# Decoder block on one core: in the opening stage, the first half's gates move behind three of its four query projections, and four idle products are put ahead of the first transposes

## The chip, the cores and the metric

The kernel runs on one core of a Trainium2 chip. The metric is the device time of one execution in microseconds (us), the median over several executions. The engines of the core that matter here are TensorE (PE in the profile; its weight loads are PEld), VectorE (DVE), ScalarE (ACT), GpSimd (POOL) and SyncE (SP, which issues most DMAs). Each runs its own instructions strictly in the order in which the program issues them to it, and waits for the others through semaphores.

## The reference

One pre-norm decoder layer with three residual branches, in float32, for x of 4 x 1024 x 512 and a context of 4 x 1024 x 384, with 16 heads of 32:

```python
x = x + attn(layernorm(x))            # "phase 0" of the kernel
x = x + xattn(layernorm(x), ctx)      # "phase 1"
x = x + ffn(layernorm(x))

# attn, the part that matters here (x is already normalized):
aperture   = sigmoid(x @ Wa + ba)     # 512 -> 16, one gate per query and head
expression = sigmoid(x @ We + be)     # 512 -> 16, one gate per key and head
inner = x @ Wi ;  outer = x @ Wo ;  v = x @ Wv        # 512 -> 512 each: queries, keys, values
a = softmax(inner . outer / sqrt(32))
a = a * aperture[query] * expression[key] ;  a = a / (a.sum + 1e-8)
y = ((a @ v), rotated and scaled by head) @ Wout
```

Only the preparation of the first of the four batches (its normalization, transposition, gates and projections) is in question. Everything after it is computed as before.

## The kernel before

The work is cut into eight units: phase 0 (self-attention) for the four batches, then phase 1 (cross-attention and feed-forward) for the four. Every unit handles 1024 tokens in two halves of 512 (`hf` = 0 and 1). `pre(u)` makes the preparation of a unit as lists of small steps: `x` (load a half of the input), `ln` (layernorm of a half), `xT` (load it back transposed), `tr` (finish the transposition), `k`, `q`, `v` (projections; the keys use the weight named Wo, the queries Wi, the values Wv), `g` (gates) and `gt` (transposition of the gates). `attention(u, hf)` gives the main steps of a unit (scores, exponentials, product with the values), and `run` mixes the preparation of the next unit between them. No scheduler reorders anything: the order of the lists is the order of each engine's queue (`tc.manual_schedule`).

The first unit has no attention to be mixed into, so its preparation runs alone. It is the list `first`, at the end of `moderate_path`, and that is the place of the change. Its steps, in the order of before:

- `p["x"][0]`: the first half of batch 0, `x0`, whose loads are issued at the very start (L137), with the four quarters of the key weights (`wk0`). `by_quarters` (L92) loads a 512 x 512 weight as four DMAs of 256 KB, one for each slice `c` of the contraction; a projection takes the slices in the order 0 to 3.
- `p["ln"][0]`: layernorm in place on `x0`: statistics (L392, L393), reciprocal root by integer arithmetic (`rsqrt`, L286 to L295), and the four normalizations (L299), one for each tile of 128 tokens. All on DVE.
- `p["x"][1]`: the load of the second half (L374). Ahead of it POOL copies a few values of the first half's root into the target (L373), so the load starts only when the root is there.
- `ahead(0, "q")`, `load_gates`, `ahead(0, "v")`, `load_biases`: the loads of Wi, of the gates' weights (`wae`, eight DMAs of 8 KB; `nbae`, eight small ones), and of Wv on SP's queue, in this order, and the biases and feed-forward weights on POOL's queue.
- `p["tr"][0]`: the first half is transposed on TensorE, by products with the identity (`across`, L321), and copied back by DVE (L280). It is the only half so treated. Every later half goes by DRAM: `away` writes the normalized rows (L303, `rows_d`), `back` reads them with rows and columns exchanged in blocks (L308, `xT`), and DVE transposes within the blocks (L314).
- `p["k"][0]`, then `negate` (DVE changes the sign of the gates' bias `nbae`, L152) and `p["g"][0]`: the gates. 16 small products (L467) with `wae`, the exponential on ACT (L473), one addition on DVE (L474), and four writes of the apertures to DRAM (L476, `iap_d`).
- `weave(p["ln"][1], p["q"][0])`: the four groups of the first half's queries (`proj`, products at L87), with the steps of the second half's layernorm set evenly between them. The two writes of `rows_d` (L303) are part of this layernorm.
- `p["gt"][0]`: SP reads the apertures back (L484, `iap`; it must wait for `iap_d`), PE transposes the gates (L488), DVE takes reciprocals (L493).
- `p["xT"][1]`: SP's four loads of the second half's transposed rows (L308); they wait for `rows_d`.
- `p["v"][0][0:3] + p["tr"][1] + p["v"][0][3:]`: the values of the first half (L87), with DVE's transpositions (L314) of the second half behind the third of four.
- `p["k"][1]`, `p["g"][1]`, `p["q"][1]` and `p["v"][1]`: the same for the second half, then the first attention step (L570).

A projection of one group of 128 columns is 16 products (32 matmul records); its result lies in one of two PSUM banks (`bank()`, a pool of two), so a third group waits until the first was copied out.

Of the kernel before, what the change touches and what calls it, by code (L numbers as in the profile page):

```python
# [42 lines left out]
@with_exitstack  # L43
def decoder_kernel(ctx: ExitStack, tc: tile.TileContext, a: dict, out: bass.AP):

    nc = tc.nc
    keep = ctx.enter_context(tc.tile_pool(name="keep", bufs=1))
    flag = keep.tile([1, 1], I32, name="flag")
    E = mybir.EngineType
    with tc.manual_schedule(engines={E.PE, E.DVE, E.Activation, E.Pool, E.SP}):
        moderate_path(tc, a, out, flag)
    again = nc.values_load(flag[0:1, 0:1], min_val=0, max_val=1, skip_runtime_bounds_check_because="0 or 1")
    with tc.If(again > 0):  # L60
        general_path(tc, a, out)


def moderate_path(tc: tile.TileContext, a: dict, out: bass.AP, flag: bass.AP):
    nc = tc.nc
    x = a["x"]
    with ExitStack() as st:
# [12 lines left out]
        def bank():  # L80
            return pf.tile([P, HALF], F32, tag="f", name="f")
# [22 lines left out]
        ident = const.tile([P, P], F32, name="ident")  # L104
# [28 lines left out]
        x0 = p2.tile([P, 4, D], F32, tag="inT", name="xin")  # L133
# [780 lines left out]
        def weave(light, items):  # L914

            first, second = sum(light, []), sum(items, [])
            out, done = [], 0
            for n, f in enumerate(first):
                upto = (2 * n + 1) * len(second) // (2 * len(first))
                out += second[done:upto] + [f]  # L920
                done = upto
            return [out + second[done:]]
# [20 lines left out]
        def one(f):  # L943
            return [[(0, f)]]
# [4 lines left out]
        def ahead(u, what):  # L949

            return one(lambda: pres[u]["load"](what))
# [62 lines left out]

        p = pres[0]
        S[0]["wk"] = wk0
        first = p["x"][0] + p["ln"][0] + p["x"][1] + ahead(0, "q") + one(load_gates) + ahead(0, "v") + one(load_biases)
        first += p["tr"][0] + p["k"][0] + one(negate) + p["g"][0]
        first += weave(p["ln"][1], p["q"][0]) + p["gt"][0] + p["xT"][1] + p["v"][0][0:3] + p["tr"][1] + p["v"][0][3:]
        first += p["k"][1] + pres[1]["x"][0] + one(load_rotations) + ahead(1, "k") + p["g"][1]  # L1020
        first += weave(pres[1]["ln"][0], p["q"][1][0:3]) + pres[1]["xT"][0] + one(angles) + p["q"][1][3:]
        first += one(load_wout) + one(rotations) + p["gt"][1]
# [15 lines left out]
        o, ln, b, tr, s = ([part for item in tail[k] for part in item] for k in ("o", "ln", "b", "tr", "s"))  # L1038
# [670 lines left out]
```

## Time and profile before

| | |
|---|---|
| time, median of 3 runs | 2247.48 us (2246.14 to 2248.22) |
| the profiled execution | 2244.28 us |
| its span in the profile | 2242.5 us |
| mean granted TensorE clock | 0.992 |
| PE busy | 2185.6 us, 97% of the span |
| DVE busy | 1569.7 us, 70% |
| ACT busy | 1238.0 us, 55% |
| first projection (keys, first half) starts | 17.87 us |
| first gates start on PE | 40.28 us |
| keys of the second half start on PE | 72.22 us |
| first scores (L570) | 115.59 us |

A row of a timeline gives the start and the length of a group of like instructions on one engine, its line, operation, tiles (out<-in) and shape, how many there were, and in brackets how long the engine was idle ahead of them and what ended the wait. A row of the stretches' table gives, for a stretch of the span, its length and mean idle-free time of each engine with the number of instructions, the TensorE clock that was granted (1.00 is full speed), the mean busy share of the 16 DMA engines, and the rate in GB/s. The trace also holds the moment at which each DMA's semaphore was raised by each DMA engine that took part in it; where the text speaks of a landing, it is the last of these. An SP row is the issue of a transfer, not its landing.

### The profile page before, as it was taken

What the parts mean: (1) busy time and instruction counts of PE and PEld (TensorE: products, weight loads), DVE (VectorE), ACT (ScalarE), POOL (GpSimd) and SP (SyncE); (2) the same over time, 40 slices, a digit from 0 to 9 for tenths busy, and PEclk for the clock granted to TensorE, in tenths of its full rate; (3) what the DMA queues carried; (4) which work ended last, traced back from release to release, by engine and by line L of the source; (5) the groups of instructions that cost most, each with busy time, mean ns of one, the idle gap of its engine ahead of it and who ended that gap; (6) DMA issues with size and microseconds to landing.
All of it is one profiled execution on the core that took longest, in us unless ns stands there. A gap on an engine that the chain in (4) does not pass through costs nothing.

```text
span 2242.5 us, 52755 instructions
## 1 busy us (share of the span) xinstructions
PE 2185.6 (97%) x22590; PEld 552.0 (25%) x22590; DVE 1569.7 (70%) x2498; ACT 1238.0 (55%) x1488; POOL 143.5 (6%) x145
## 2 busy tenths in 40 slices
PE   6999999999999999999999999999999999999995
PEld 2322222222222222222222222222222222222222
DVE  3468676797766967567686666868777787856576
ACT  0055545555455554555556565565756566577673
POOL 4000011000000000000000000101000010101010
PEclk9999999999999999999999999999999999999997
DMA  4422223122231221211413032221223142203131
GB/s 112 134 80 50 69 89 106 34 79 69 88 104 35 78 69 46 71 52 41 120 32 104 33 86 63 77 82 45 77 80 103 44 105 68 78 21 102 34 87 40
DMA packets 153305, 161.71 MB, mean 72 GB/s; under 512 B 46202, under 2 KB 91898, under 8 KB 151908
## 3 DMA queue, kind: packets, MB, share of 16 engines
q1 hardware_dynamic: 150380, 156.20, 23.9%
q8 instruction: 179, 2.93, 0.6%
q0 software_dynamic: 2144, 0.98, 0.3%
q10 hardware_dynamic: 536, 1.05, 0.1%
q14 instruction: 66, 0.54, 0.1%
HBM read 115.40 MB, written 42.74 MB: 71 GB/s over the span
## 4 chain that ended last, share of the span: by engine, by line
PE 85%; DVE 6%; ACT 3%; issue 2%; DMA 2%; SPq 1%; DVEq 0%; ACTq 0%; POOL 0%
PE f L87 32%; PE s L570 23%; PE av L597 19%; PE sm L605 6%; DVE es L583 3%; PE sm L627 3%; ACT e L575 2%; SPq L92 1%; DVE g L860 1%; PE f L871 1%; PE f L837 1%; ACT hid L854 1%; DMA sum_d<-both 1%; DMA rec_d<-rec 0%; DVE xT L314 0%
## 5 line engine op out<-in xcount | busy, mean ns | idle before, releaser
L575 ACT ACTIVATE e<-s 128x1024 f32<-128x1024 f32 x1024 | 994.2, 1022 | 716.9 <-PE s L570 534.5
L583 DVE TENSOR_TENSOR es<-es,e 128x1024 f32<-128x1024 f32 x534 | 653.6, 1249 | 277.1 <-ACT e L575 276.6
L570 PE MATMUL s<-q,k 32*64 32x512 f32 x8192 | 620.7, 613 | 7.1 <-ACT e L575 5.4
L597 PE MATMUL av<-e,v 128*32 128x512 f32 x4096 | 554.1, 603 | 0.0
L87 PE MATMUL f<-xT,w 128*32 128x512 f32 x2816 | 331.5, 592 | 0.0
L591 DVE SCALAR_TENSOR_TENSOR eg<-e,sw,eg 128x512 f32<-128x512 f32 x448 | 318.5, 746 | 2.3
L570 PEld LDWEIGHTS s<-q,k 32*64 32x64 f32 x8192 | 136.9, 129 | 459.9 <-ACT e L575 256.6
L581 DVE TENSOR_TENSOR es<-e 128x1024 f32<-128x1024 f32 x89 | 109.5, 1253 | 189.3 <-ACT e L575 181.6
L87 PE MATMUL f<-w,q 128*32 128x512 f32 x1984 | 238.2, 592 | 0.4 <-DVE q L716 0.4
L597 PEld LDWEIGHTS av<-e,v 128*32 128x32 f32 x4096 | 88.5, 108 | 403.8 <-issue 401.1
L87 PEld LDWEIGHTS f<-xT,w 128*32 128x32 f32 x2816 | 92.8, 110 | 210.7 <-issue 203.2
L605 PE MATMUL sm<-e,sw 128*2 128x512 f32 x1024 | 133.3, 592 | 0.0
L774 POOL TENSOR_TENSOR r<-res,bo_bc 128x512 f32<-128x512 f32 x32 | 40.9, 1278 | 1085.2 <-DVE res L766 823.1
L87 PE MATMUL f<-w,xT 128*32 128x512 f32 x896 | 104.9, 592 | 0.6 <-DVE q L280 0.6
L87 PEld LDWEIGHTS f<-w,q 128*32 128x32 f32 x1984 | 65.4, 110 | 149.6 <-issue 143.8
L87 PE MATMUL f<-ctxT,w 128*32 128x512 f32 x768 | 92.3, 592 | 0.0
L87 PE MATMUL f<-w,ctxT 128*32 128x512 f32 x768 | 91.9, 592 | 0.0
L854 ACT ACTIVATE hid<-sT,units 128x256 f32<-128x256 f32 x128 | 76.2, 603 | 23.0 <-DVE g L860 20.2
L627 PE MATMUL sm<-es,ones 128*1 128x512 f32 x348 | 69.0, 591 | 3.9 <-DVE es L583 3.6
L822 POOL TENSOR_TENSOR res<-res,bout_bc 128x512 f32<-128x512 f32 x28 | 59.6, 2136 | 76.9 <-DVE r L299 76.9
L860 DVE SCALAR_TENSOR_TENSOR g<-hid,units,g 128x256 f32<-128x256 f32 x120 | 57.6, 480 | 9.2 <-ACT hid L854 3.8
L677 DVE TENSOR_TENSOR q<-both,recb 128x512 f32<-128x512 f32 x63 | 46.3, 735 | 25.0 <-DMA recb<-rec_d 24.8
(254 smaller groups left out, 1064.9 us busy)
## 6 DMA issues: line engine op xcount, KB each, us to landing
recb<-rec_d SPq DMA_DIRECT2D x252, 64.0 KB
xT<-rows_d SPq DMA_DIRECT2D x60, 256.0 KB
rows_d<-r SPq DMA_DIRECT2D x60, 256.0 KB
w<-in_xattn_Wo SPq DMA_DIRECT2D x9, 1024.0 KB
w<-wout_d SPq DMA_DIRECT2D x8, 1024.0 KB
res<-in_x SPq DMA_DIRECT2D x32, 256.0 KB
x1b_d<-r SPq DMA_DIRECT2D x32, 256.0 KB
res<-x1b_d SPq DMA_DIRECT2D x32, 256.0 KB
```

Source lines behind the costliest of these rows:

```text
L87: nc.tensor.matmul(to[r], lhsT=lhsT[:, j, :] if len(lhsT.shape) == 3 else lhsT[:, r], rhs=rhs, **flags)
L570: nc.tensor.matmul(s[m : m + 64, j, :], lhsT=k[r, g, kt * P + m : kt * P + m + 64], rhs=q[r, g, :], start=True, stop=True,)
L575: nc.scalar.activation(e, s, AF.Exp, scale=SCALE)
L581: nc.vector.tensor_tensor(me["es"][i], me["e", 0][i], es[i], ALU.add)
L583: nc.vector.tensor_tensor(me["es"][i], me["es"][i], es[i], ALU.add)
L591: nc.vector.scalar_tensor_tensor(eg, es[0][:, h, :], gate(kt), eg, ALU.mult, ALU.add)
L597: nc.tensor.matmul(av[r, :], lhsT=me["v"][:, kt, HG * g + h, :], rhs=es[h // 2][:, h % 2, :], start=(kt == 0), stop=(kt == NT - 1),)
L605: nc.tensor.matmul(sm[j * DH : j * DH + sums, :], lhsT=me["sw"][:, t, HG * g + 2 + h, :] if ph == 0 else ones, rhs=me["e", t][1][:, h, :], ...
L627: nc.tensor.matmul(sm[j * DH : j * DH + 1, :], lhsT=ones, rhs=e, start=True, stop=True)
L822: return lambda: nc.gpsimd.tensor_tensor(res[t], res[t], bout_bc, ALU.add)
L854: nc.scalar.activation(hid, res["s"], AF.Relu, bias=units[:, 1, h : h + 1], scale=units[:, 0, h : h + 1])
L860: nc.vector.scalar_tensor_tensor(res["g"], res["hid"], units[:, 2, h - 1 : h], res["g"], ALU.mult, ALU.add)
```

## The change

Two edits in the list `first`. The gates of the first half (`negate` and `g[0]`) are moved behind the third of the four query groups; all steps of the second half's layernorm, which were spread over four query groups, are now spread over these three, so they all stand ahead of `negate` and `g[0]`. The fourth query group follows the gates. And a new step `warm` stands between the load of `x0` and its layernorm: four products of the identity with the raw tiles of `x0`, into a PSUM bank that nobody reads.

```diff
         p = pres[0]
         S[0]["wk"] = wk0
-        first = p["x"][0] + p["ln"][0] + p["x"][1] + ahead(0, "q") + one(load_gates) + ahead(0, "v") + one(load_biases)
-        first += p["tr"][0] + p["k"][0] + one(negate) + p["g"][0]
-        first += weave(p["ln"][1], p["q"][0]) + p["gt"][0] + p["xT"][1] + p["v"][0][0:3] + p["tr"][1] + p["v"][0][3:]
+
+        def warm():
+
+            idle = bank()
+            for i in range(4):
+                nc.tensor.matmul(idle, lhsT=ident, rhs=x0[:, i, :], start=True, stop=True)
+
+        first = p["x"][0] + one(warm) + p["ln"][0] + p["x"][1] + ahead(0, "q") + one(load_gates) + ahead(0, "v") + one(load_biases)
+        first += p["tr"][0] + p["k"][0] + weave(p["ln"][1], p["q"][0][0:3]) + one(negate) + p["g"][0] + p["q"][0][3:]
+        first += p["gt"][0] + p["xT"][1] + p["v"][0][0:3] + p["tr"][1] + p["v"][0][3:]
         first += p["k"][1] + pres[1]["x"][0] + one(load_rotations) + ahead(1, "k") + p["g"][1]
```

## The prediction

> **What bounds the kernel now.** I read the page's first part, then the opening in the timelines of PE, SP and DVE, the stretches' table for the clock and the DMA share, and last the recorded landings.
>
> ```profile
> span 2242.5 us, 52755 instructions
> PE 2185.6 (97%) x22590; PEld 552.0 (25%) x22590; DVE 1569.7 (70%) x2498; ACT 1238.0 (55%) x1488; POOL 143.5 (6%) x145
> ```
>
> PE is busy for 97%. Every stage after the opening starts when PE is through with the one before, so a shift of the opening's end is carried to the end of the span one for one. The opening on PE:
>
> ```profile
> 11.81 5.24 PE L321 MATMUL f<-ident,xin 128*32 128x128 f32 x128 [11.81 <-DVE xin L299]
> 17.87 13.94 PE L87 MATMUL f<-xin,w 128*32 128x512 f32 x128 [0.81 <-DVE xin L280]
> 40.28 1.94 PE L467 MATMUL f<-xin,wae 128*32 128x128 f32 x32 [8.47 <-DMA wae<-in_attn_We]
> 41.96 15.66 PE L87 MATMUL f<-xin,w 128*32 128x512 f32 x128
> 58.44 13.94 PE L87 MATMUL f<-w,xin 128*32 128x512 f32 x128 [0.55 <-DVE q L280]
> 72.22 13.94 PE L87 MATMUL f<-xT,w 128*32 128x512 f32 x128
> ```
>
> These are transposes, keys, gates, queries, values, and the second half's keys. One hole of 8.47 us stands ahead of the gates, and the queries took 15.66 us where the other projections took 13.94. The table tells why: the granted clock is half after the hole.
>
> ```profile
> 30.00:35.00 5.00, 1.81 (x20) 0.30 (x12) 0.69 (x1) 0.00 (x0) 4.65 (x8) 1.00 0.32 93
> 35.00:36.00 1.00, 0.00 (x0) 0.00 (x0) 0.00 (x0) 0.00 (x0) 0.54 (x2) 0.61 0.34 90
> 40.00:45.00 5.00, 4.72 (x48) 2.35 (x52) 0.08 (x1) 0.00 (x0) 0.00 (x0) 0.50 0.08 4
> 45.00:46.00 1.00, 1.00 (x12) 0.31 (x8) 0.08 (x1) 0.85 (x1) 0.00 (x0) 0.77 0.26 29
> 50.00:55.00 5.00, 5.00 (x52) 1.62 (x48) 4.55 (x19) 0.00 (x0) 0.00 (x0) 1.00 0.28 103
> ```
>
> The other thing to see in it is the DMA column. While a weight arrives (30 to 35, 50 to 55) the rate is some 100 GB/s and 0.26 to 0.34 of the 16 engines are busy: about four of them carry a `by_quarters` load. SP's issues and the second half's transposition:
>
> ```profile
> 11.85 12.70 SPq L92 DMA_DIRECT2D w<-in_attn_Wi  x4
> 43.67 2.51 SPq L92 DMA_DIRECT2D w<-in_attn_Wv  x4
> 47.10 3.56 SPq L476 DMA_DIRECT2D iap_d<-gi  x4
> 54.84 1.89 SPq L303 DMA_DIRECT2D rows_d<-xin  x2
> 58.70 0.36 SPq L484 DMA_DIRECT2D iap<-iap_d  x1
> 60.49 1.93 SPq L308 DMA_DIRECT2D xT<-rows_d  x4
> 69.63 2.49 DVE L314 STREAM_TRANSPOSE xT<-xT 128x512 f32<-128x512 f32 x4
> ```
>
> Issue is early, landing late. The recorded landings: Wi's slices 29.43, 32.68, 35.45, 38.32; Wv's 49.10, 52.60, 55.21, 57.81; `rows_d` 59.16 and 60.43; the last quarter of `xT` 69.55. So the values (58.44) started 0.6 us after their last slice, and the second half's keys (72.22) came 0.1 us after DVE's transposition (72.12), which began 0.08 us after `xT` was there. Behind the hole, the transfers leave no slack.
>
> **The change part by part.**
>
> *Gates out of the way.* The hole's work does not vanish: the queries that come forward need Wi, whose last slice lands at 38.32. The keys end at 31.8. A slice of a group is 13.94 / 16 = 0.87 us. Slices 0 and 1 fill 31.8 to 33.6, slice 2 runs from 35.5, slice 3 from 38.4 to 39.3. Three groups less one are 6.9, gates 1.1 (the second half's took 1.08), the fourth group 3.4: queries and gates end at 50.7, against 57.55. Saved there: 6.9 us at full clock. If the clock falls in these gaps, up to half of the 5.2 us that it stayed low after 40.28 is lost, 2.6 us, and the end is 53.3. The gates' ACT and DVE steps (1.28 us table load, 0.37, 0.23) hide behind the fourth group; without that cover they would cost 1.9 us. `negate` now waits on DVE behind the third group's copy, which ends after the bias is there (44.92). POOL issues nothing in the moved steps, and no load changes its place.
>
> *The values.* Wv is issued by SP at 43.67, behind the gates' eight weight and eight bias DMAs, whose order is not touched; so its last slice still lands near 57.8. A fetch of PE's instructions (16 KB, 1.05 us at 48.31 on one of the four engines) delayed one engine: on the other three the slice had landed by 56.83. With the gates elsewhere in PE's stream this fetch moves out of Wv's time; I take 56.9. Values then end at 56.9 + 0.1 + 0.9 + 3 x 3.4 = 68.2 instead of 72.2. This is the most that the change can bring: 4.0 us.
>
> *The second half's rows.* Its layernorm moves forward from 47-56 to 32-45 (x had landed at 25.79), its two `rows_d` writes now stand ahead of the four `iap_d` writes on SP, and are issued at 46.2, right behind Wv, 8.6 us sooner. That does not help them. `iap_d`, issued at 47.1 to 50.7, had twelve of its sixteen shares landed by 51.68 and the last four at 57.3 to 58.56, after Wv: on the four engines a transfer waits for what SP issued earlier. `rows_d` has a share there too, and took 1.3 us for each of its two writes after Wv had ended. So they land at 56.8 + 2.6 = 59.4, or at 60.4 to 60.6 if the next fetch (1.3 us; its place in PE's stream is now the end of the first group of values, some 58 us) falls among them. The rule for this is the Trainium skill's, "DMA: Bandwidth & Descriptors", sections on queues, rings and completion order and on why a semaphore counts to 16: each engine takes a queue's descriptors in ring order, and a transfer uses the largest count up to 16 that divides its slowest dimensions, the lowest-numbered engines first. It speaks against the change, and the landings agree with it (four shares late). By the rule the gain is near nothing; without it, with `rows_d` landing 2.7 us after issue as on the other twelve engines, it would be the 4.0 of the step before.
>
> *A new order of waits on SP.* `iap` waits for `iap_d`, and `xT` stands behind `iap`. `iap_d` now lies behind `rows_d` on the four engines: after 59.4 to 60.5, four landings at 0.19 apart, then 0.36 for `iap`'s issue. `xT` is issued at 60.5 to 61.7, against 60.49. From issue to landing it took 9.06 us, 7.46 on the engines that the second fetch (62.75, 1.33 us) missed. With one fetch instead of two in the whole stretch, `xT` lands between 68.0 and 69.6; in the middle, with the fetch among `rows_d`: 61.7 + 7.46 = 69.2. With both the late issue and a fetch in it: 70.8, the bad end. DVE adds 2.57, and the second half's keys start at 71.8 (70.6 to 73.4), against 72.22: 0.4 us sooner. A stall of PE takes the place of the hole: 68.2 to 71.8 if the clock was full.
>
> *Idle products.* Sixteen records more on PE. Four full 128x128x512 products took 3.7 us (L229), at half clock some 7: from 5.5 to 9 or 12.5, where PE only waited. They read what DVE normalizes from 11.17 on: if only the tile in use is protected, no wait; if all of `x0` is, up to 1.4 us. They may bring 1.5: the transposes' first 55 records ran at 53 ns until the clock rose at 14.7, the rest at 27. But the keys' third slice landed at 18.79, so the keys start no sooner than 17.2 to any use, and Wi's last slice (38.32) takes even those 0.7 us. Both ends are covered: 0. Uncovered they would be worth -0.7 to +1.4.
>
> *Sum.* Queries -6.9, of which 4.0 pass the wait for Wv, of which 0.4 pass `xT`; idle products 0. Against the profiled 2244.28 that is 2243.9; the median of the runs lies 3.2 above it, so 2247.48 - 0.4 = 2247.1.
>
> **The rivals.**
>
> 1. *Faster: `xT` is in time*, because its chain is not held by the four engines. For it: twelve engines are free from 46 on. Against it: `iap_d`'s last shares. The values then set the end: 68.2 instead of 72.2, 2243.5; half of it if only the fetches fall well, 2245.5.
> 2. *Slower: the clock falls in the new stalls.* PE now waits in pieces at 53 to 57 and again ahead of the second half's keys. The first is covered: values that start at half clock lose up to 2.6 us of the 3.6 that they would wait anyway. The second is not. The price is 1.7 to 2.6 us, as after 40.28, and decides from a wait of about 3.4 us (31.8 to 35.2 was enough). With `xT` at the bad end (+1.2) it makes 2250 to 2251.3. The Trainium skill, "TensorE: Matmul & The Clock Gate", part on the activity monitor, has free-running windows of 3413 ns; the falls and rises here at 14.73, 35.21 and 45.45 are six and three such windows apart. By it a wait of 3.6 us would fill one window only in a lucky phase, and the loss would mostly be avoided.
> 3. *The change does nothing*: transfers hold everything, 2247.5. This lies within 0.4 us of my forecast and is counted with it.
>
> **How the numbers follow.** My case, within 1.5 us of 2247.1: 0.55 (2245.6 to 2248.6). Rival 1: 0.22; rival 2: 0.23. The range takes in the full 4.0 of the first and 2251 of the second, since the three runs spread by 2.1: 2243.3 to 2250.8. A change of 0.2%, 4.5 us, is about what a measurement of this kernel tells from none. The bound of 4.0 lies inside it, so faster needs Wv to land sooner too, 0.08; slower needs both parts of rival 2 and more, 0.07; within, 0.85.
>
> **What would show it.** After the change: queries start at 31.8 with gaps that a DMA of w<-in_attn_Wi ends; no wait on in_attn_We; values' first group waits for w<-in_attn_Wv until 57 to 58; `rows_d` issued at 46 to 49, `xT` still at 60 to 62; the second half's keys at 70.6 to 73.4 behind DVE xT. Transposes at full clock from the start, keys some 0.7 us sooner. It is wrong if Wv lands well before 56.8, if `xT` is issued before 59, or if the half clock lasts into the second half's projections.

## The result

| | before | after |
|---|---|---|
| median of 20 runs each | 2248.01 us (2244.55 to 2250.86) | 2245.48 us (2243.88 to 2248.09) |
| ratio after / before | | 0.9991, 95% interval 0.9984 to 0.9997 |
| the profiled execution: span | 2242.5 us | 2245.0 us |
| first half's keys start | 17.87 us | 16.84 us |
| second half's keys start | 72.22 us | 70.89 us |
| first scores | 115.59 us | 115.95 us |

By the ratio the change makes the kernel 2.0 us faster (0.7 to 3.6; the two medians lie 2.5 apart), 0.09%: small, but the 95% interval stays below 1. It is far below the 8.47 us of the hole that is filled. The two profiled executions stand the other way round; most of that, 2.2 us, lies behind the first scores, where the two kernels run the same instructions (see the repeated runs below).

The opening after the change, in the timeline of PE:

```profile
5.63 5.99 PE L1022 MATMUL f<-xin,ident 128*128 128x512 f32 x8 [5.63 <-DMA xin<-in_x]
16.84 15.11 PE L87 MATMUL f<-xin,w 128*32 128x512 f32 x136 [0.81 <-DVE xin L280]
32.13 1.06 PE L87 MATMUL f<-xin,w 128*32 128x512 f32 x8 [0.19 <-DMA w<-in_attn_Wi]
34.89 1.06 PE L87 MATMUL f<-xin,w 128*32 128x512 f32 x8 [1.70 <-DMA w<-in_attn_Wi]
37.99 9.41 PE L87 MATMUL f<-xin,w 128*32 128x512 f32 x72 [2.04 <-DMA w<-in_attn_Wi]
47.23 1.05 PE L467 MATMUL f<-xin,wae 128*32 128x128 f32 x32
56.91 11.37 PE L87 MATMUL f<-w,xin 128*32 128x512 f32 x104 [1.45 <-DMA w<-in_attn_Wv]
70.89 15.64 PE L87 MATMUL f<-xT,w 128*32 128x512 f32 x128 [2.61 <-DVE xT L314]
```

The one wait on in_attn_We is gone. In its place stand waits for single slices of Wi, then of Wv, and one for DVE's transposition of `xT`. What is behind that last one stands in the timelines of SP and DVE:

```profile
46.18 3.19 SPq L303 DMA_DIRECT2D rows_d<-xin  x2
50.25 1.78 SPq L476 DMA_DIRECT2D iap_d<-gi  x4
60.14 0.38 SPq L484 DMA_DIRECT2D iap<-iap_d  x1
60.63 2.03 SPq L308 DMA_DIRECT2D xT<-rows_d  x4
68.30 2.49 DVE L314 STREAM_TRANSPOSE xT<-xT 128x512 f32<-128x512 f32 x4 [2.69 <-DMA xT<-rows_d]
```

`rows_d` is issued 8.7 us sooner than before, and `xT` 0.14 us later. Of the sixteen shares of the two writes, twelve had landed by 50.5 and 51.8 us, the other four of each at 58.0 and 59.3, just after Wv's last slice (56.87). And the second half's keys, 1.33 us sooner at their start, run at half clock for a while: they take 15.64 us instead of 13.94. The table of stretches shows the fall:

```profile
65.00:70.00 5.00, 3.27 (x32) 0.78 (x24) 2.31 (x4) 0.00 (x0) 0.00 (x0) 1.00 1.11 275
70.00:75.00 5.00, 4.11 (x24) 1.41 (x28) 1.36 (x3) 0.00 (x0) 0.00 (x0) 0.67 0.09 24
```

### The profile page after: what moved, and what is told of

It is laid out like the page before. It is cut to its first block, busy times and chain, and to the rows that moved or that the text cites. A ratio compares the mean times of both kernels' runs of the same rounds, so it can differ in the third digit from the quotient of the medians.

```text
span 2245.0 us, 52774 instructions
## 1 busy us (share of the span) xinstructions
PE 2192.7 (98%) x22598; PEld 551.4 (25%) x22598; DVE 1570.0 (70%) x2498; ACT 1237.8 (55%) x1488; POOL 143.2 (6%) x145
## 4 chain that ended last, share of the span: by engine, by line
PE 81%; DVE 6%; DMA 4%; ACT 3%; issue 3%; SPq 2%; DVEq 0%; ACTq 0%; POOL 0%
PE f L87 30%; PE s L570 23%; PE av L597 18%; PE sm L605 6%; DVE es L583 3%; PE sm L627 2%; ACT e L575 2%; SPq L92 1%; DMA sum_d<-both 1%; DMA rec_d<-rec 1%; DVE g L860 1%; PE f L871 1%; PE f L837 1%; DMA xT<-rows_d 1%; ACT hid L854 1%
```

## The experiments

The theory: the opening's end hangs on transfers. A weight cut by slices of the contraction runs on four of the sixteen DMA engines, and everything that SP issues later waits for its share on these four. Its rivals: the warmed clock brings the gain; or PE's own order of work does; or the rate of the queue as a whole is the limit.

All profiled executions beside each other (us). The last column is the span less the first scores, a stretch in which none of these kernels was edited:

| kernel | 2nd half's keys start | they take | first scores | rest |
|---|---|---|---|---|
| before | 72.22 | 13.94 | 115.59 | 2126.9 |
| before, again | 71.87 | 13.94 | 115.24 | 2126.7 |
| after | 70.89 | 15.64 | 115.95 | 2129.0 |
| after, again | 70.42 | 15.64 | 115.48 | 2126.6 |
| idle products alone | 71.93 | 13.94 | 115.30 | 2130.9 |
| gates moved alone | 70.86 | 15.64 | 115.93 | 2132.1 |
| after, `xT` ahead of `iap` | 71.39 | 13.94 | 114.76 | 2129.2 |
| after, clock kept | 70.91 | 13.94 | 114.28 | 2130.8 |
| after, Wi and Wv spread | 65.81 | 13.94 | 109.18 | 2130.6 |
| before, Wi and Wv spread | 68.50 | 13.94 | 111.87 | 2130.5 |
| after, rows on ACT's queue | 73.39 | 13.94 | 116.75 | 2130.8 |
| after, all three weights spread | 60.23 | 13.94 | 103.60 | 2128.1 |
| before, all three weights spread | 62.52 | 13.94 | 105.89 | 2126.5 |

The rest varies by 5.6 us from execution to execution, more than the change is worth. It does not vary evenly. Set beside each other instruction by instruction, the distance between two executions changes by 0.3 us at most from 150 to 1500 us behind the first scores; they part at a few places. One lies between 63 and 106 us behind the first scores: there after loses 1.7 us against after, again, the same program. Another is a wait of PE on ACT, 1.2 to 1.3 us, at 1954 to 1972 us of the span in twelve of the thirteen. In five of them the granted clock fell to half right behind it (idle products alone, `xT` ahead of `iap`, clock kept, and after with two and with three weights spread); these lose 1.5 us there, 2.8 where the clock stayed low for 6.83 us (clock kept), and the others nothing. So the experiments are read by the first scores, and the times stand beside them.

### The two parts of the change, each alone

The idle products alone, against the kernel before:

```diff
+        def warm():
+
+            idle = bank()
+            for i in range(4):
+                nc.tensor.matmul(idle, lhsT=ident, rhs=x0[:, i, :], start=True, stop=True)
+
-        first = p["x"][0] + p["ln"][0] + p["x"][1] + ahead(0, "q") + one(load_gates) + ahead(0, "v") + one(load_biases)
+        first = p["x"][0] + one(warm) + p["ln"][0] + p["x"][1] + ahead(0, "q") + one(load_gates) + ahead(0, "v") + one(load_biases)
```

The gates moved alone is the changed kernel without these lines:

```diff
-        first = p["x"][0] + one(warm) + p["ln"][0] + p["x"][1] + ahead(0, "q") + one(load_gates) + ahead(0, "v") + one(load_biases)
+        first = p["x"][0] + p["ln"][0] + p["x"][1] + ahead(0, "q") + one(load_gates) + ahead(0, "v") + one(load_biases)
```

> The four idle products alone, the gates left where they were. Transfer theory (the opening's end is set by the landing of the transposed rows, xT, which hangs on Wv's four DMA engines): transposes run at full clock, the first half's keys start some 1 us sooner (near 16.8 us instead of 17.87), the hole ahead of the gates grows by as much, the second half's keys start at 72.2 to 72.7 as before; time within 1 us of before. Rival (the measured 2 us come from the warmed clock): the second half's keys start 1 to 2 us sooner and the time is 2 us below before, the whole of the change's gain.

> The gates moved, without the idle products. Transfer theory: all of the change's gain; queries wait for the slices of Wi until 38, values for Wv until 57, xT issued near 60.6 us, the second half's keys start at 70.5 to 71.3 us, and the time is 1 to 3 us below before (as the whole change). Rival (idle products needed): second half's keys at 72 or later, no gain.

Measured: idle products alone 0.9994 of before (0.9985 to 1.0003), gates alone 0.9998 (0.9989 to 1.0007). Neither interval excludes no change, nor the whole change's 0.9991; the times don't tell the parts apart, and the 1 to 3 us that the gates alone were expected to bring are not seen (0.4 us, between 2.5 less and 1.6 more). The openings do. With the idle products alone:

```profile
16.84 1.92 PE L87 MATMUL f<-xin,w 128*32 128x512 f32 x16 [0.82 <-DVE xin L280]
18.92 12.22 PE L87 MATMUL f<-xin,w 128*32 128x512 f32 x112 [0.16 <-DMA w<-in_attn_Wo]
39.96 1.94 PE L467 MATMUL f<-xin,wae 128*32 128x128 f32 x32 [8.81 <-DMA wae<-in_attn_We]
```

the keys start 1.03 us sooner, wait at once for their own weight's third slice, and end in a hole that is 0.34 longer. The second half's keys come at 71.93, between the 71.87 and the 72.22 of the kernel before. With the gates alone everything from the gates on (47.21 against 47.23) is as in the changed kernel, the start and the half clock of the second half's keys too, and the first scores come at 115.93 against 115.95:

```profile
70.86 15.64 PE L87 MATMUL f<-xT,w 128*32 128x512 f32 x128 [2.54 <-DVE xT L314]
```

So the earlier start of the second half's keys comes from the gates' move, and so does the fall of the clock that uses it up; in the opening the idle products change nothing that is left over.

### `xT` issued ahead of the apertures' read

```diff
-        first += p["gt"][0] + p["xT"][1] + p["v"][0][0:3] + p["tr"][1] + p["v"][0][3:]
+        first += p["xT"][1] + p["gt"][0] + p["v"][0][0:3] + p["tr"][1] + p["v"][0][3:]
```

> The changed kernel with the loads of xT issued ahead of the read of the apertures (iap) on SP. In the changed kernel the rows had landed at 59.28 us, but xT was issued at 60.63, behind iap, which waits for iap_d (59.99). Transfer theory: xT issued at 59.4, landed at 66.9 to 67.2, the second half's keys at 69.5 to 69.8 us instead of 70.89; 1.2 us less than the changed kernel, some 3 us below before if the clock does as before. Rival (values or PE set the start of the second half's keys): the start stays at 70.9.

Measured: 0.9988 of before (0.9979 to 0.9997), and the second half's keys at 71.39, not at 69.6. The edit did what it should, and something else went wrong in that execution. SP's timeline:

```profile
44.68 2.64 SPq L92 DMA_DIRECT2D w<-in_attn_Wv  x4
47.44 3.12 SPq L303 DMA_DIRECT2D rows_d<-xin  x2
60.92 1.92 SPq L308 DMA_DIRECT2D xT<-rows_d  x4
```

`xT` was issued 0.02 us after the rows' landing (60.90), where in the changed kernel 1.35 us passed (59.28 to 60.63). So the read of the apertures does cost its 1.3 us. But Wv was issued at 44.68 instead of 43.55: the issue of one of the gates' bias loads, which stand ahead of it on SP, took 1.42 us where the others took 0.42. It began at 42.29, as a fetch of instructions did; that the fetch was the cause is not shown. Wv's last slice came at 58.50 instead of 56.87, and the rest with it. That lateness is about what the expected start was missed by; the two waits in a row, Wv and the rows, agree with the expectation.

### The clock kept through the wait

```diff
+        def keep():
+            idle = bank()
+            for i in range(2):
+                nc.tensor.matmul(idle, lhsT=ident, rhs=x0[:, i, :], start=True, stop=True)
-        first += p["gt"][0] + p["xT"][1] + p["v"][0][0:3] + p["tr"][1] + p["v"][0][3:]
+        first += p["gt"][0] + p["xT"][1] + p["v"][0][0:3] + p["tr"][1] + one(keep) + p["v"][0][3:]
```

> The changed kernel with two more idle products of 0.85 us ahead of the last group of the first half's values, where PE otherwise waits 2.6 us for xT. Transfer theory with a clock that falls in that wait: the second half's keys start at 70.9 as in the changed kernel, since xT sets it, but run at full clock, 13.94 us instead of 15.64; the second half's gates start at 84.7 instead of 86.3; time up to 1.7 us below the changed kernel, 0 in executions in which the clock did not fall. Rival (PE is the bound there): the second half's keys start 1.7 us later and the time is 1.7 us above the changed kernel.

Measured: 0.9984 of before (0.9975 to 0.9993). The timeline of PE:

```profile
64.69 1.98 PE L1028 MATMUL f<-xin,ident 128*128 128x512 f32 x4
66.60 3.64 PE L87 MATMUL f<-w,xin 128*32 128x512 f32 x32
70.91 13.94 PE L87 MATMUL f<-xT,w 128*32 128x512 f32 x128 [0.67 <-PE f L87]
84.64 1.08 PE L467 MATMUL f<-xT,wae 128*32 128x128 f32 x32
```

The start is that of the changed kernel to 0.02 us, although PE did 1.9 us of idle work ahead of it (64.69 to 66.60), and the keys then run at full clock: first scores 1.67 us sooner. So PE is not the bound there, the wait is real, and it costs a second time through the clock.

### The loads spread over all DMA engines

```diff
-                if which in ("q0", "k0", "v0", "q1"):
+                if which in ("q0", "v0") and which not in spread:
+                    spread.append(which)
+                    for q in range(NC):
+                        nc.sync.dma_start(w[ts(q, NB)], src.rearrange("(q c i) f -> q i c f", c=NC, i=NB)[q])
+                elif which in ("q0", "k0", "v0", "q1"):
```

> The changed kernel, with Wi and Wv of the first unit cut by partitions instead of by slices of the contraction: four loads of 32 partitions x 4 slices each, so that a load's slowest dimension is 32 and not 4. Same bytes, same count, same place in SP's queue. Transfer theory (a load cut by slices runs on four of the sixteen DMA engines, 10.4 us for 1 MB, and everything behind it waits on those four): all sixteen engines share it, Wv lands within 3 to 4 us of its issue, Wi before 30 us, the rows at 44 to 46; no wait of PE from 19 us on, queries 31 to 46, values from 47, the second half's keys at 60.5 us instead of 70.9, first scores near 104 instead of 116; time 11 to 12 us below before (2236 to 2237). Rival (the rate of one queue or of memory is the limit, not the four engines): Wv still takes some 10 us, nothing moves, time as the changed kernel.

> The kernel before, with the same cut of Wi and Wv. Transfer theory: the gates' weights no longer lie behind 10 us of Wi; they land near 30 us, so the hole ahead of the gates is gone without moving them; queries 33 to 47, second half's keys at 61 to 62 us; time within 1 us of the changed kernel with the same cut, 10 to 12 us below before. So moving the gates is then worth 0 to 1 us. Rival (the gates stand in the way by their own chain: bias, table load, exponential): the hole stays at 5 us or more, and the kernel is 5 us slower than the changed one with the same cut.

Measured: 0.9964 (0.9952 to 0.9975) on the changed kernel, 2240.20 us, 8 us below before where 11 to 12 were expected; 0.9986 (0.9977 to 0.9995) on the kernel before, 2244.27 us, 3 us below where 10 to 12 were expected. Wv was issued at 39.45 and its four parts landed at 42.6, 44.1, 45.7 and 47.9: 8.5 us from issue to the last landing, where the slices took 13.3. All sixteen engines raised its semaphore, against four before, and the rows, no longer held back on four of them, landed at 50.6 instead of 59.3. So the four engines were the limit and the rival falls. But 8.5 us are more than the 3 to 4 expected, and far from a quarter of 13.3: something else paces the new cut, and what it is was not looked into. And nearly half of the expected 12 us at the first scores stayed out, since Wi landed at 34.3 and not before 30:

```profile
16.77 1.92 PE L87 MATMUL f<-xin,w 128*32 128x512 f32 x16 [0.81 <-DVE xin L286]
19.00 12.22 PE L87 MATMUL f<-xin,w 128*32 128x512 f32 x112 [0.31 <-DMA w<-in_attn_Wo]
34.58 12.20 PE L87 MATMUL f<-xin,w 128*32 128x512 f32 x96 [3.36 <-DVE bnmv L399]
```

(The wait of 3.36 us is put down to DVE, as the one that came last by the profile; no statistic is an input of the queries, and Wi had landed 0.24 us earlier.) The keys' weight was still loaded by slices and held the four engines until 19, the second half's input had its last shares there at 28.4, and Wi, now on all sixteen, had its own last shares behind those. On the kernel before, the hole was expected to vanish and shrank only to 4.93 us:

```profile
36.60 1.93 PE L473 MATMUL f<-xin,wae 128*32 128x128 f32 x32 [4.93 <-DMA wae<-in_attn_We]
38.28 15.64 PE L87 MATMUL f<-xin,w 128*32 128x512 f32 x128
```

With this cut, the change is worth 2.7 us at the first scores, and 4.1 us in the medians (the idle products stay covered in it: its keys wait for their own weight until 19.00). That expectation failed, as the other did; that the cause is the same, the keys' weight on its four engines, is shown below, where this weight is spread too and the hole is gone.

### The rows on another queue

```diff
-        def away(rows, xt, t, n):
-            nc.sync.dma_start(rows[t : t + n].rearrange("t p d -> p t d"), xt)
+        def away(rows, xt, t, n, dma=nc.sync.dma_start):
+            dma(rows[t : t + n].rearrange("t p d -> p t d"), xt)
...
+                                nc.scalar.dma_start if u == 0 else nc.sync.dma_start,
```

> The changed kernel with the two writes of the first unit's normalized rows issued by ScalarE instead of SP: another queue on the same DMA engines. If order within SP's queue holds the rows back: their last four shares land by 49 to 53 us, some 3 us after issue, instead of 58.0 and 59.3, and Wv's last slice lands up to 2.6 us later, at 57 to 59.5, since the same four engines carry both. If the four engines are simply full, whatever the queue: the last shares still land after 57. In both cases xT is hardly issued sooner than 60, as it stands behind the apertures' read, and these remain on SP behind Wv.

Measured, in one profiled execution: the rows, issued at 47.04 and 47.91, had their twelve shares landed by 49.8 and 51.1, the last four at 54.3 and 57.0; Wv's slices, 2.6 us apart otherwise, came 3.7 and 4.4 us apart meanwhile, and the last landed at 60.74. Wv itself was issued 0.9 us later than in the changed kernel (44.48). Neither side of the expectation is met cleanly: the rows pass Wv, so SP's order did hold them back, but their late shares come 2.6 us apart where they took 1.3 alone, so the four engines are also full. The landings agree with the Trainium skill, "DMA: Bandwidth & Descriptors", section on queues, rings and completion order: an engine takes one queue's descriptors in order, and takes turns between the queues that have work for it. The values now set the end:

```profile
60.78 12.77 PE L87 MATMUL f<-w,xin 128*32 128x512 f32 x104 [1.48 <-DMA w<-in_attn_Wv]
73.39 13.94 PE L87 MATMUL f<-xT,w 128*32 128x512 f32 x128
```

with the second half's keys 2.5 us later than in the changed kernel. What is gained for the rows is taken from Wv.

### All three weights of the first unit spread

```diff
-        by_quarters(queues, wk0, W_IN["k0"][0])
+        for q in range(NC):
+            queues[q % 2](wk0[ts(q, NB)], W_IN["k0"][0].rearrange("(q c i) f -> q i c f", c=NC, i=NB)[q])
```

> The changed kernel with the keys' weight of the first unit cut by partitions too, beside Wi and Wv. With Wi and Wv alone, PE still waited 3.36 us for Wi (landed 34.34), since the keys' weight held the four engines until 19 and the second half's input until 28. Transfer theory: keys' weight lands by 9, the second half's input by 18, Wi by 24, Wv by 36; PE has no wait for a transfer from 12 us on, keys 16.8 to 30.6, queries and gates to 45.3, values 46 to 59.8, second half's keys at 59.8, first scores near 103 (116 in the changed kernel); time 12 to 13 us below before, 5 to 6 below the kernel with Wi and Wv alone. Rival (by then something else, the layernorm's chain or SP's many small loads, sets the end): first scores stay above 107.

> The kernel before with the same three cuts. Transfer theory: the gates' weights land by 28, ahead of the keys' end at 31.6, so the hole ahead of the gates is gone, and the order of gates and queries hardly matters: first scores at 103.5 to 105, within 1.5 us of the changed kernel with the same cuts, 11 to 12 us below before. Rival (the gates' place matters by itself): first scores 3 us or more behind that kernel.

Measured: 0.9955 (0.9942 to 0.9969) on the changed kernel, 2235.49 us; 0.9959 (0.9945 to 0.9972) on the kernel before, 2236.95 us. That is 10 and 9 us below before, a little short of the 12 to 13 and 11 to 12 expected, and these two beat both kernels. The changed kernel with the three cuts, on PE:

```profile
16.96 24.24 PE L87 MATMUL f<-xin,w 128*32 128x512 f32 x224 [0.81 <-DVE xin L287]
41.02 1.06 PE L474 MATMUL f<-xin,wae 128*32 128x128 f32 x32
46.47 13.94 PE L87 MATMUL f<-w,xin 128*32 128x512 f32 x128 [0.55 <-DVE q L287]
60.23 13.94 PE L87 MATMUL f<-xT,w 128*32 128x512 f32 x128
```

and the kernel before with the same:

```profile
19.25 13.94 PE L87 MATMUL f<-xin,w 128*32 128x512 f32 x128 [0.81 <-DVE xin L287]
33.00 1.06 PE L474 MATMUL f<-xin,wae 128*32 128x128 f32 x32
62.52 13.94 PE L87 MATMUL f<-xT,w 128*32 128x512 f32 x128
```

From the first keys on there is no wait for a transfer in either: 43.27 us from the first half's keys to the second's in both (60.23 - 16.96, 62.52 - 19.25), gates first or last. So the gates' place is worth nothing once their weights are there in time. What is left between the two, 2.29 us at the first scores where at most 1.5 were expected, are the idle products, which are now uncovered: the transposes of the second ran at half clock until 17.6 us, and its keys started that much later.

### Both kernels once more

> The kernel before once more, for a second profile: if the difference between the two first profiles (span 2242.5 before, 2245.0 after, against medians the other way) lies behind the opening and is chance, the stretch from the first scores to the end comes out at 2129 to 2132 us here, not at 2126.9; the first scores at 115 to 116.5.

> The changed kernel once more, for a second profile: xT issued near 60.6 and the second half's keys at 70.7 to 71.2 us unless the bias's small loads are late; these keys take 13.9 us where the clock holds and 15.6 where it falls, so the first scores come at 114.2 or at 115.9; the stretch behind them 2127 to 2132 us.

Measured: first scores at 115.24 and 115.48, rest 2126.7 and 2126.6 us. The kernel before was expected to show a longer rest this time and did not. The kernel after showed 2129.0 in one execution and 2126.6 in the other, as little as before, so the 2.2 us by which the first profile of after was longer behind the opening are not shown to be the change's. In the second one the second half's keys came a little ahead of the 70.7 to 71.2 expected:

```profile
70.42 15.64 PE L87 MATMUL f<-xT,w 128*32 128x512 f32 x128 [2.65 <-DVE xT L314]
```

In both profiles of after the clock fell in these keys, and the opening ended 0.24 to 0.36 us later than before's, for 1.33 and 1.45 us gained at these keys' start.

## Why the prediction was right, step by step

- *Bound*: right. Transfers, not PE, set the opening's end: spreading three loads brought the first scores 12.4 us forward on the changed kernel, while moving the gates had brought the second half's keys 1.3 to 1.5. That a shift of the opening is carried to the end one for one also holds where it is large enough to be seen: before with three weights spread had its first scores 9.4 to 9.7 sooner and its time 9.2 lower.
- *Gates out of the way*: right. Queries waited for Wi's slices until 37.99 (38.4 foretold), the clock fell in the gaps, and queries and gates ended at 51.8, between 50.7 and 53.3.
- *The values*: right. Last slice of Wv at 56.87 (56.9), values' end at 68.3 (68.2). The instruction fetch did move out of Wv's time.
- *The rows*: right, but for the fetch. Issued at 46.18, landed at 59.28 (59.4 without the fetch among them, which is what came: at 57.88 it delayed none of the four shares). I had taken the case with it.
- *SP's order of waits*: right. `iap` 60.14, `xT` 60.63 (60.5 to 61.7), 7.59 us to landing (7.46).
- *Second half's keys*: 70.89, inside 70.6 to 73.4, but 0.9 sooner than the middle that I took, for the fetch. The step's 0.4 measured 1.33 (1.45 against the second profile of each).
- *Idle products*: right that they are covered. Their uncovered worth was mis-sized: keys 1.03 us sooner, not 0.7, and 2.2 sooner than in the second profile of before, where the clock rose at 17.44 instead of 14.73 and the keys started at 19.05. With all weights spread it was 2.29.
- *Rival 2, the clock*: this is the step that failed, although it came out inside its price. I let it decide from a wait of 3.4 us, gave it 0.23, and put the fall of the clock at nothing in the sum; a wait of 2.61 was enough, in both profiles of after and in the gates alone. It cost 1.70 (1.7 to 2.6 foretold), and used up what the second half's keys had gained. With it came one of the signs that I had set for being wrong: the half clock stood in the second half's keys, from 71.75 to 75.16. The rule that I set beside it, free-running windows of 3413 ns (the Trainium skill, "TensorE: Matmul & The Clock Gate", on the activity monitor), holds for when the clock changes: at 10.31, 37.62, 41.03, 71.75 and 75.16 in the profile of after, whole windows apart. But I read from it that a whole window must be idle. The windows that ended in a fall were in part busy: 0.86 of 3.41 us in the one that ended at 71.75. There the measurement decides.
- *The sum*: -0.4 us foretold; the ratio gives -2.0 (-0.7 to -3.6). The measured 2245.48 lies 0.1 below the band of my case and next to the half gain of rival 1 (2245.5), but rival 1's reason, `xT` in time, did not come. The range that I stated takes in no change as well, so it tells little. The profiles' openings give +0.2 to +0.4 with the fall of the clock, and would give -1.3 to -1.5 without it; that the time fell all the same is not what my steps add up to, and there I was lucky. Part of it may be the clock of the whole run: the granted clock was 0.9935 on average in the 20 runs of after, and 0.9924 to 0.9929 in the three sets of the kernel before that were timed with the experiments, 62 runs; by a straight line through these the span is some 1.5 us shorter for each 0.001 (correlation -0.7). And the gates alone, with the same opening as after from the gates on, ran at 0.9927 and gained almost nothing. This doesn't separate the causes; where the 2.0 us come from stays open.

## What to carry to other kernels

A hole in the busiest engine is worth what the next wait leaves of it: look up when the last input of each following step lands before moving work into the hole. If a transfer's rate is a fraction of what others reach at the same time, look at the shape of its slowest dimension, since the engines that carry it hold back all that is issued behind it; here another cut of three loads, without the reordering, gave over four times the change's gain, 9 us against 2, and made the reordering needless. Idle work that keeps the clock up pays just where a wait on something else stands ahead of a stage that then runs uncovered.

## What the runs showed of the hardware that I had not expected

The clock falls without a fully idle stretch. Reckoned by the granted clock's own steps of 3.41 us, windows in which PE was busy for about a quarter (the wait for `xT` in after) or a third (queries' slices in after, 1.06 of 3.41) ended in half clock. The busy share alone doesn't decide it: in the gates alone a window busy for 44% (34.05 to 37.47) ended in half clock, while with `xT` ahead of `iap`, where the windows lay otherwise in the same gaps, two that were busy for 45% and 43% (32.92 to 39.75) did not, and the clock held through the whole opening. Behind one and the same wait of 1.2 to 1.3 us, far from the edits, it fell in some executions and not in others. A single fetch of instructions, 16 KB and about 1 us on one DMA engine, can delay a whole weight: in before Wv's last slice had landed on three engines by 56.83, and on the fourth, some 1 us behind since a fetch at 48.31, at 57.81; in after, with the fetch elsewhere, all four were through at 56.87. And spans of one and the same stretch of 2130 us varied by 5.6 us between executions, which hid effects of 1 to 2 us that the timelines show plainly.
